# An attention and feed-forward kernel on one core: doubled temporaries and split down products in the last quarter, the weight flag made earlier, reciprocals moved to cycle heads

## The chip, the core and the metric

The kernel runs on one NeuronCore of one Trainium2 chip. A core has five engines with instruction queues of their own, worked off in order: TensorE (PE in the profile; its weight loads are listed apart as PEld), VectorE (DVE), ScalarE (ACT), GpSimd (POOL) and SyncE (SP), which here does nothing but start DMA transfers. Operands lie in SBUF, 128 partitions wide; TensorE writes its sums into eight PSUM banks of 128 x 512 fp32 each. The metric is device time in microseconds (us), the median of several runs.

## The reference

Two sequences of 1024 rows by 512 go through one layer with normalisation after each half. Cut to what matters:

```python
Q = (x @ Wq.T + bq)   # 32 heads of 16
K = (x @ Wk.T + bk)   # 8 heads of 16, each for 4 heads of Q
V = (x @ Wv.T + bv)
Q, K = _rope(Q, K)
scores = einsum('bhqd,bhkd->bhqk', Q, K) / sqrt(16)
attn = einsum('bhqk,bhkd->bhqd', softmax(scores), V)
x = _layernorm(x + attn @ Wo.T + bo)
g = einsum('th,ih->ti', x, gate_w) * gate_s      # 512 -> 1408
u = einsum('th,ih->ti', x, up_w) * up_s
hdn = silu(g) * u
x = _layernorm(x + einsum('ti,hi->th', hdn, down_w) * down_s)
```

The three feed-forward matrices hold -1, 0 and 1; the kernel checks at run time that its weights lose nothing in the matmul format, and has a general feed-forward for others.

## The kernel before, in words

**Units, steps, cycles.** The attention is cut into 32 units: sequence, half of the query rows, and group of four heads (`g`, 0 to 7). A unit has 8 steps. The main loop takes two steps at a time, so it makes 128 passes, called cycles here; a quarter (one sequence, one half of its rows) is 8 units, or 32 cycles. Operands of the score matmuls are split into a high and a low part in the matmul format, so each product is made of two matmuls.

**Two passes over the scores.** The maximum of each row of scores is needed before the exponentials. `max_pass` (L333) makes the scores once for the maximum, which VectorE takes out of a `pa` bank (L341), 12 steps ahead. `max_rows` combines these for a unit (L347 to L353: four small VectorE operations) and sends them through DRAM (L356, L359) into `mt`. `exp_pass` (L370) makes the scores again, transposed, with a third matmul that subtracts the maximum, and ScalarE takes the exponential (L378). `av` (L389) multiplies by the values, with a column of ones beside each, so that it yields numerators and denominators. After a unit's last step `unit_out` (from L399) copies the sum out, and two DMAs (L412, L413) put it into `num` and `den`. After every second unit (odd `g`) the reciprocals of `den` are taken in four pieces of 128 columns (L417), and `num` is multiplied by them (L418).

**The order.** The engines' order is written out by hand. Lists of letters (L649 to L656) say for one cycle where TensorE makes a piece of a max pass (A), of an exp pass (B), a step's value product (V, twice), and a filling block (F, at the head of a cycle): a projection with rope, or a piece of an earlier quarter's output projection or feed-forward. Cycles without a filling block use another list, and the last ones have no max pass. The four `pa` banks serve the max pass and the filling blocks by turns. `after(n, f)` puts `f` aside until n steps later; it is then issued at a V, ahead of that step's value product, in the midst of the cycle's maxima. Weight pieces are rounded and checked in the first cycles (`piece_round`, L167), at the head of a cycle.

**The weight flag.** `piece_round` gathers the low bits of all weights into `low` (the last in cycle 18). `low_flag` (L179) reduces them, sends the 128 results of 4 bytes to DRAM (`fl`, L184), back as one row (`flr`, L185), and four steps later reduces that to `flag` (L186), which is read when all else is done. `low_flag` is called at the end of cycle 26, after the load of the down weights `wd_sb` (L712, 2.8 MB) and of five weight tiles `wt` (L440) have been put on SP's queue, and before the loads `xq` of the residual rows (L429). The operand loads of a unit (`prep`, L310: KS, QH, QL) follow on the same queue at the end of every fourth cycle, three units ahead.

**A quarter's feed-forward.** Its blocks are two of `project` (two row tiles each, L463), two of `x1_turn`, then for each of 11 chunks of 128 hidden columns a gate and an up product (`hidden`, L504), then `down` for each of four row tiles (L546: 22 matmuls over the 11 chunks). A chunk's elementwise chain is: ScalarE `th` = tanh (L519) and `z` (L520); VectorE `z` = (th + 1) z (L523); ScalarE `pus` (L529), which takes the buffer of `th`; GpSimd `z` = pus z (L532); then the split into `hh` and `hl`. All of `th`, `z` and `pus` have a single buffer. Three quarters' feed-forwards fill the cycles of later attention; the last stands alone behind the loop, with eight PSUM banks, and there the split is made by ScalarE (L534) and VectorE (L535). Its `down` is followed by L555, L556, the sums (L448, L449), two small GpSimd operations (L451, L452), the norm (L458) and the store (L567).

Of the kernel before, what the change touches and what calls it, by code (L numbers as in the profile page):

```python
# [7 lines left out]
F32 = mybir.dt.float32  # L8
# [8 lines left out]
P = 128  # L17
# [29 lines left out]
def attn_ffn_kernel(tc, x, wqkv, bqkv, wo, bo, rope, wg, wu, wd, gs, us, ds, out):  # L47
    nc = tc.nc

    def pool(name, bufs=1, **kw):  # L50
        return tc.alloc_tile_pool(name=name, bufs=bufs, **kw)
# [3 lines left out]
    dram2 = pool("dram2", 2, space=DRAM)  # L55
    ap1 = pool("ap1")
    ap2 = pool("ap2", 2)
    ap3 = pool("ap3", 3)
    ap4 = pool("ap4", 4)
    wp = pool("wp", RING, side="right")  # L60
    qp1 = pool("qp1", side="right")
    qp2 = pool("qp2", 2, side="right")
# [123 lines left out]
        after(4, lambda: nc.vector.tensor_reduce(flag, flr, AX.X, ALU.max))  # L186

    later = {}
    now = [0]

    def after(n, f):
# [207 lines left out]
    def unit_out(u):  # L399


        b, qh, g = UNITS[u]
        q = u // HKV
        o = ap1.tile([P, HALF], F32, tag="o", name="o")
        nc.scalar.copy(o, PV.pop(u))
        if g % 2 == 0:
            NUM[q, g // 2] = ap4.tile([P, HALF], F32, tag="num", name="num")
            NUM["den"] = ap1.tile([P, HALF], F32, tag="den", name="den")
        num, den = NUM[q, g // 2], NUM["den"]
        r0 = (g % 2) * G * HD  # L410
        rows = slice(r0, r0 + G * HD)
        nc.sync.dma_start(out=num[rows, :], in_=o[0:P:2, :])  # L412
        nc.sync.dma_start(out=den[rows, :], in_=o[1:P:2, :])  # L413
        if g % 2:
            for k in range(TH):
                ns = slice(k * P, (k + 1) * P)
                after(min(k + 1, TH - 1), lambda ns=ns: nc.vector.reciprocal(den[:, ns], den[:, ns]))  # L417
            after(TH, lambda: nc.vector.tensor_tensor(num, num, den, ALU.mult))  # L418


    XQ, FP = {}, {}
# [76 lines left out]
    def hidden(q, f, up):  # L498
        i = (q * NF + f) * 2 + up
        w = WT.pop(i)  # L500
        p = bank("pg")
        for c in range(NC):
            for k, x1 in enumerate(FP["x1"]):
                nc.tensor.matmul(  # L504
                    p,
                    w[:, c, :],
                    x1[:, c, :],
                    start=c == 0 and k == 0,
                    stop=c == NC - 1 and k == 1,
                )  # L510
        ask_weights(i + RING - 1)
        if not up:
            if f == 0:
                FP["h"] = [
                    fp1.tile([P, NF, HALF], F32R, tag=f"h{i}", name=f"h{i}") for i in "hl"
                ]
            th = fp1.tile([P, HALF], F32, tag="th", name="th")
            z = FP["z"] = fp1.tile([P, HALF], F32, tag="z", name="z")
            nc.scalar.activation(th, p, AF.Tanh, scale=gs2[:, f : f + 1])  # L519
            nc.scalar.mul(z, p, gs2[:, f : f + 1])  # L520

            after(
                1, lambda: nc.vector.scalar_tensor_tensor(z, th, 1.0, z, ALU.add, ALU.mult)  # L523
            )
            return
        hi, lo = (h[:, f, :] for h in FP["h"])
        z = FP["z"]
        pus = fp1.tile([P, HALF], F32, tag="th", name="pus")
        nc.scalar.mul(pus, p, ust[:, f : f + 1])  # L529

        def rest():
            nc.gpsimd.tensor_tensor(z, pus, z, ALU.mult)  # L532
            if q == LASTQ:
                nc.scalar.copy(hi, z)  # L534
                nc.vector.tensor_tensor(lo, z, hi.bitcast(F32), ALU.subtract)  # L535
            else:
                nc.gpsimd.tensor_copy(hi, z)
                nc.gpsimd.tensor_tensor(lo, z, hi.bitcast(F32), ALU.subtract)

        after(1, rest)  # L540

    def down(q, t):
        pd = bank("pd")
        for f in range(NF):
            for k, h in enumerate(FP["h"]):
                nc.tensor.matmul(  # L546
                    pd,
# [2 lines left out]
                    start=f == 0 and k == 0,  # L550
                    stop=f == NF - 1 and k == 1,
                )
        ys = fp1.tile([P, D], F32, tag="ys", name="ys")
        if q == LASTQ:
            nc.vector.tensor_tensor(ys, pd, dsb, ALU.mult)  # L555
# [37 lines left out]
    def quarter(q):  # L593
# [3 lines left out]
        for f in range(NF):  # L597
            for up in (0, 1):
                fs.append(lambda a=(q, f, up): hidden(*a))
        for t in range(TH):  # L600
            fs.append(lambda t=t: down(q, t))
        return [(first, f) for f in fs]

    PHASES = 4 + 2 * NF + TH
# [59 lines left out]
    for c in range(STEPS // 2):  # L664
# [4 lines left out]
            piece_round(i)  # L669
        if pieces:  # L670
            after(1, lambda ps=pieces: [(piece_store(i), piece_load(i + 4)) for i in ps])
        alone = 2 * c + LEAD >= STEPS
        has_fill = bool(fill) and fill[0][0] <= c
        if c >= (STEPS - QS) // 2:
# [25 lines left out]
            prep(u + 3)  # L700
        if (2 * c + 1 + LEAD) % US == US - 1 and not alone:
            max_rows((2 * c + 1 + LEAD) // US)
        if c == QS // 2 - 6:
            sp4.release()
            qp4.release()
# [6 lines left out]
            nc.sync.dma_start(  # L712
                out=wd_sb.bitcast(F32), in_=wsd[2 * NF : PIECES].rearrange("f p n -> p f n")
            )
            ask_weights(RING - 1)
            low_flag()
            for t in range(TH):
                load_residual(0, t)
            for q in range(B * NH - 1):
# [1 line left out]
    for n, prob in sorted(before.items()):  # L721
        v_hook(n + 2)
        av(n, prob)
    for p in (ps_v, ps_b, ps_a[0]):
        p.release()
    ps_x = pool("ps_x", 8, space=PSUM)
    psf[0] = (ps_x, "px")

# [17 lines left out]
    fill += last[4:]  # L746
    drain()
    order.__exit__(None, None, None)
    for p in (ps_x, fp5, fp2, fp1, wp, ap4, ap3, ap2, ap1):
        p.release()  # L750
    general = nc.values_load(flag[0:1, 0:1])
    with tc.If(general != 0):
# [120 lines left out]
```

## Time and profile before

| what | us |
|---|---|
| median of 3 runs (lowest, highest) | 1245.93 (1244.38, 1246.58) |
| the profiled execution, its own time | 1244.49 |
| its span, first to last instruction | 1242.4 |
| TensorE busy | 1170.1 |
| VectorE busy | 872.4 |
| ScalarE busy | 704.7 |
| GpSimd busy | 354.1 |
| mean granted TensorE clock | 0.969 of full |

The profile is of one execution; its times are counted from the start of its span. An engine's idle time counts only where another that sets the end waits for it. The views used are the page (engine shares), the list of waits (who waited for whom), the timeline (instructions in order of time, with the idle time before each and what released it) and the view by stretches (busy time of each engine between two times, with the clock granted to TensorE). L with a number is a line of the kernel before.

### The profile page before, as it was taken

What the parts mean: (1) busy time and instruction counts of PE and PEld (TensorE: products, weight loads), DVE (VectorE), ACT (ScalarE), POOL (GpSimd) and SP (SyncE); (2) the same over time, 40 slices, a digit from 0 to 9 for tenths busy, and PEclk for the clock granted to TensorE, in tenths of its full rate; (3) what the DMA queues carried; (4) which work ended last, traced back from release to release, by engine and by line L of the source; (5) the groups of instructions that cost most, each with busy time, mean ns of one, the idle gap of its engine ahead of it and who ended that gap; (6) DMA issues with size and microseconds to landing.
All of it is one profiled execution on the core that took longest, in us unless ns stands there. A gap on an engine that the chain in (4) does not pass through costs nothing.

```text
span 1242.4 us, 22712 instructions
## 1 busy us (share of the span) xinstructions
PE 1170.1 (94%) x8784; PEld 606.5 (49%) x8784; DVE 872.4 (70%) x1492; ACT 704.7 (57%) x1300; POOL 354.1 (29%) x340
## 2 busy tenths in 40 slices
PE   7799999999799999999999999999999999999876
PEld 5344435454344454545444454546444454455664
DVE  4578898878677878785568878784867878703324
ACT  2026757566555766765446676763547776762350
POOL 3126351530103222224421222225331222245321
PEclk9679999999899999999999999999999999999897
DMA  5457776433411222221312222221212222111420
GB/s 159 130 190 252 249 233 237 155 132 122 135 44 61 79 79 81 93 78 52 99 48 67 82 92 84 84 78 44 79 60 87 78 78 79 45 61 43 136 60 36
DMA packets 82291, 126.80 MB, mean 102 GB/s; under 512 B 15873, under 2 KB 29442, under 8 KB 82050
## 3 DMA queue, kind: packets, MB, share of 16 engines
q1 hardware_dynamic: 82178, 125.30, 31.6%
q8 instruction: 71, 1.16, 0.4%
q14 instruction: 42, 0.34, 0.1%
HBM read 80.43 MB, written 36.44 MB: 94 GB/s over the span
## 4 chain that ended last, share of the span: by engine, by line
PE 62%; DVE 21%; POOL 5%; DMA 4%; issue 3%; ACT 3%; SPq 1%; POOLq 0%; DVEq 0%; ACTq 0%
PE pb L370 14%; PE pv L389 13%; DVE mx L341 12%; PE pa L333 11%; PE pg L504 10%; PE pq L241 5%; PE pd L546 5%; PE py L463 3%; DVE den L417 3%; POOL z L532 1%; DVE st L448 1%; DMA fl<-red 1%; POOL xq L561 1%; POOL ys L560 1%; DVE z L523 1%
## 5 line engine op out<-in xcount | busy, mean ns | idle before, releaser
L341 DVE TENSOR_REDUCE mx<-pa 128x1 f32<-128x512 f32 x1024 | 643.2, 681 | 187.8 <-PE pa L333 185.6
L378 ACT ACTIVATE prob<-pb 128x512 f32<-128x512 f32 x1024 | 544.5, 599 | 274.1 <-PE pb L370 263.0
L333 PE MATMUL pa<-KS,QH 32*128 32x512 f32 x1024 | 365.8, 470 | 41.7 <-DVE mx L341 23.8
L333 PE MATMUL pa<-KS,QL 32*128 32x512 f32 x1024 | 349.1, 432 | 0.0
L370 PE MATMUL pb<-QH,KS 32*128 32x512 f32 x1024 | 321.7, 477 | 1.0 <-ACT prob L378 1.0
L389 PE MATMUL pv<-prob,va 128*32 128x512 f32 x2048 | 275.5, 610 | 0.0
L370 PE MATMUL pb<-QL,KS 32*128 32x512 f32 x1024 | 270.6, 423 | 0.0
L370 PE MATMUL pb<-mt,ones 32*128 32x512 f32 x1024 | 254.5, 395 | 0.0
L333 PEld LDWEIGHTS pa<-KS,QH 32*128 32x128 f32 x1024 | 154.0, 186 | 168.7 <-DVE mx L341 144.2
L532 POOL TENSOR_TENSOR z<-pus,z 128x512 f32<-128x512 f32 x44 | 56.2, 1277 | 462.7 <-ACT pus L529 462.7
L370 PEld LDWEIGHTS pb<-QH,KS 32*128 32x128 f32 x1024 | 134.9, 182 | 82.5 <-issue 48.9
L370 PEld LDWEIGHTS pb<-QL,KS 32*128 32x128 f32 x1024 | 125.6, 184 | 85.6 <-issue 85.5
L333 PEld LDWEIGHTS pa<-KS,QL 32*128 32x128 f32 x1024 | 163.3, 188 | 5.4 <-DMA QL<-qT 0.5
L370 PEld LDWEIGHTS pb<-mt,ones 32*128 32x128 f32 x1024 | 140.6, 184 | 23.7 <-issue 15.9
L504 PE MATMUL pg<-x1h,wt 128*128 128x512 f32 x352 | 146.5, 416 | 0.7 <-ACT x1h L493 0.7
L504 PE MATMUL pg<-x1l,wt 128*128 128x512 f32 x352 | 139.5, 396 | 0.3 <-DVE x1l L494 0.3
L389 PEld LDWEIGHTS pv<-prob,va 128*32 128x32 f32 x2048 | 40.8, 108 | 93.9 <-issue 82.7
L504 PEld LDWEIGHTS pg<-x1h,wt 128*128 128x128 f32 x352 | 67.1, 191 | 38.0 <-issue 12.8
L546 PE MATMUL pd<-wd_sb,hh 128*128 128x512 f32 x176 | 71.8, 408 | 10.8 <-ACT hh L534 10.2
L241 PE MATMUL pq<-xT,wqkv_sb 128*128 128x512 f32 x160 | 76.7, 626 | 0.0
L504 PEld LDWEIGHTS pg<-x1l,wt 128*128 128x128 f32 x352 | 67.2, 191 | 13.1 <-DVE x1l L494 0.8
L546 PE MATMUL pd<-wd_sb,hl 128*128 128x512 f32 x176 | 70.5, 401 | 0.2 <-DVE hl L535 0.2
(80 smaller groups left out, 976.5 us busy)
## 6 DMA issues: line engine op xcount, KB each, us to landing
wt<-wsd SPq DMA_DIRECT2D x88, 256.0 KB
KS<-kT SPq DMA_DIRECT2D x128, 128.0 KB
wsd<-sr SPq DMA_DIRECT2D x33, 256.0 KB
qT<-hi SPq DMA_DIRECT2D x16, 512.0 KB
qT<-lo SPq DMA_DIRECT2D x16, 512.0 KB
QH<-qT SPq DMA_DIRECT2D x32, 256.0 KB
QL<-qT SPq DMA_DIRECT2D x32, 256.0 KB
xs<-in_x_dram SPq DMA_DIRECT2D x16, 256.0 KB
```

The source lines that it names most:

```text
L241: nc.tensor.matmul(pq, wqkv_sb[:, c, m * P : (m + 1) * P], XT[b, half][:, c, :], start=c == 0, stop=c == NC - 1,)
L333: nc.tensor.matmul(PA[n, j], (QH, QL)[i][u][r, t * P : (t + 1) * P], KS[u][r, half * HALF : (half + 1) * HALF], start=i == 0, stop=i == 1,)
L341: nc.vector.tensor_reduce(MX[u][:, t, j, half : half + 1], PA.pop((n, j)), AX.X, ALU.max)
L370: nc.tensor.matmul(PB[n, j], ones[r, :] if i == 2 else KS[u][r, kc * P : (kc + 1) * P], (QH[u], QL[u], mts[u % 2])[i][r, :], start=i == 0, ...
L378: nc.scalar.activation(prob[:, j, :], PB.pop((n, j)), AF.Exp, scale=SCALE)
L389: nc.tensor.matmul(PV[u][j * E : (j + 1) * E, :], vas[b][:, kc, g, :, :].rearrange("p d o -> p (d o)"), prob[:, j, :], start=done == 0, st ...
L417: after(min(k + 1, TH - 1), lambda ns=ns: nc.vector.reciprocal(den[:, ns], den[:, ns]))
L448: nc.vector.bn_stats(st, row)
L463: nc.tensor.matmul(py, NUM[q, c][:, t * P : (t + 1) * P], wo_sb[:, c, :], start=c == 0, stop=c == NC - 1,)
L504: nc.tensor.matmul(p, w[:, c, :], x1[:, c, :], start=c == 0 and k == 0, stop=c == NC - 1 and k == 1,)
L532: nc.gpsimd.tensor_tensor(z, pus, z, ALU.mult)
L546: nc.tensor.matmul(pd, h[:, f, t * P : (t + 1) * P], wd_sb[:, f, :], start=f == 0 and k == 0, stop=f == NF - 1 and k == 1,)
```

## The change

Three parts.

1. In the last quarter `th`, `z` and `pus` come from a new pool `tp2` with two buffers of each, and `pus` no longer takes the buffer of `th`. The pool lies where `ap3` (attention operands) lay, which is given back behind the main loop; for that `ap3` is made after `ap4`. The last `down` calls are cut: row tiles 0 and 1 first over chunks 0 to 9, then chunk 10 of each, then tiles 2 and 3 whole.
2. `low_flag` is called at the end of cycle 22 instead of cycle 26.
3. The reciprocals after an odd unit are issued at the heads of cycles, two at the second cycle after the unit's last value product, two at the third, and the product with `num` at the fourth. For the last unit of a quarter they stay at the steps: two at the first V after, two at the second, the product at the third (before: one, one, two, then the product at the fourth).

```diff
+    ap4 = pool("ap4", 4)
     ap3 = pool("ap3", 3)
-    ap4 = pool("ap4", 4)
...
         if g % 2:
+            c = now[0] // 2
             for k in range(TH):
                 ns = slice(k * P, (k + 1) * P)
-                after(min(k + 1, TH - 1), lambda ns=ns: nc.vector.reciprocal(den[:, ns], den[:, ns]))
-            after(TH, lambda: nc.vector.tensor_tensor(num, num, den, ALU.mult))
+                f = lambda ns=ns: nc.vector.reciprocal(den[:, ns], den[:, ns])
+                if g == HKV - 1:
+                    after(k // 2 + 1, f)
+                else:
+                    early.setdefault(c + 2 + k // 2, []).append(f)
+            f = lambda: nc.vector.tensor_tensor(num, num, den, ALU.mult)
+            if g == HKV - 1:
+                after(3, f)
+            else:
+                early.setdefault(c + 4, []).append(f)
...
-            th = fp1.tile([P, HALF], F32, tag="th", name="th")
-            z = FP["z"] = fp1.tile([P, HALF], F32, tag="z", name="z")
+            th = FP["tmp"].tile([P, HALF], F32, tag="th", name="th")
+            z = FP["z"] = FP["tmp"].tile([P, HALF], F32, tag="z", name="z")
...
-        pus = fp1.tile([P, HALF], F32, tag="th", name="pus")
+        pus = FP["tmp"].tile(
+            [P, HALF], F32, tag="pus" if q == LASTQ else "th", name="pus"
+        )
...
-    def down(q, t):
-        pd = bank("pd")
-        for f in range(NF):
+    def down(q, t, f0=0, f1=NF):
+        if f0 == 0:
+            FP["d", t] = bank("pd")
+        pd = FP["d", t]
+        for f in range(f0, f1):
...
+        if f1 < NF:
+            return
...
-        for t in range(TH):
-            fs.append(lambda t=t: down(q, t))
+        downs = [(t, 0, NF) for t in range(TH)]
+        if q == LASTQ:
+
+            downs[:2] = [(0, 0, NF - 1), (1, 0, NF - 1), (0, NF - 1, NF), (1, NF - 1, NF)]
+        for a in downs:
+            fs.append(lambda a=a: down(q, *a))
...
+        for f in early.pop(c, ()):
+            f()
         alone = 2 * c + LEAD >= STEPS
...
+        if c == QS // 2 - 10:
+            low_flag()
         if c == QS // 2 - 6:
...
+            FP["tmp"] = fp1
             ask_weights(RING - 1)
-            low_flag()
...
-    for p in (ps_v, ps_b, ps_a[0]):
+    for p in (ps_v, ps_b, ps_a[0], ap3):
         p.release()
+    FP["tmp"] = tp2 = pool("tp2", 2)
```

## The prediction

> **What bounds the kernel now.** I read the shares by engine first, then the list of waits, then the timeline at the places the change touches. TensorE is busy 94% of the span, so most of the time is matmul work that the change leaves alone; only what makes TensorE wait, or run at half clock, can be won.
>
> ```profile
> PE 1170.1 (94%) x8784; PEld 606.5 (49%) x8784; DVE 872.4 (70%) x1492; ACT 704.7 (57%) x1300; POOL 354.1 (29%) x340
> ```
>
> The list of waits (times in us: sum, count, longest):
>
> ```profile
> PE pa L333 <- DVE mx L341: 23.8, 33, 6.9
> PE pd L546 <- ACT hh L534: 10.2, 3, 3.5
> DVE flag L186 <- DMA flr<-fl: 8.3, 1, 8.3
> ```
>
> The reader is to see two waits of TensorE and one wait of VectorE that feeds the first: of its 23.8 us, 6.9 are one wait. I call one pass of the main loop a cycle (128 of them). A cycle ends with every eighth `mt,ones` matmul in TensorE's timeline, so the timeline gives each cycle's length.
>
> *The tail.* One chunk of the last feed-forward in the timeline (start, duration, engine, line; in brackets the idle time before it and its releaser):
>
> ```profile
> 1170.73 0.68 ACT L519 ACTIVATE th<-pg,gs 128x512 f32<-128x512 f32 x1
> 1171.58 0.69 ACT L520 ACTIVATE z<-pg,gs 128x512 f32<-128x512 f32 x1 [0.17 <-DVE hl L535]
> 1172.30 0.69 DVE L523 SCALAR_TENSOR_TENSOR z<-th,z 128x512 f32<-128x512 f32 x1 [0.76 <-ACT z L520]
> 1173.09 0.69 ACT L529 ACTIVATE pus<-pg,ust 128x512 f32<-128x512 f32 x1 [0.82 <-DVE z L523]
> 1173.92 1.29 POOL L532 TENSOR_TENSOR z<-pus,z 128x512 f32<-128x512 f32 x1 [3.75 <-ACT pus L529]
> 1175.24 0.62 ACT L534 CAST hh<-z 128x512 fp32r<-128x512 f32 x1 [1.46 <-POOL z L532]
> 1175.77 0.68 ACT L519 ACTIVATE th<-pg,gs 128x512 f32<-128x512 f32 x1
> ...
> 1206.12 0.49 PE L546 MATMUL pd<-wd_sb,hh 128*128 128x512 f32 x1 [3.19 <-ACT hh L534]
> ```
>
> A chunk takes 5.04 us here (1170.73 to 1175.77), while its 16 matmuls start 0.227 us apart and need 3.63. TensorE ends the hidden layer at 1199.15, then finds chunks 8 to 10 missing, waits, and falls to half clock.
>
> *The flag, and the middle.* First the timeline, then the view by stretches, cut at cycle ends (from:to, length, busy time of each engine, granted clock, DMA share, GB/s):
>
> ```profile
> 324.21 0.27 DVE L186 TENSOR_REDUCE flag<-flr 1x1 int32<-1x128 int32 x1 [8.27 <-DMA flr<-fl]
> ```
>
> ```profile
> 303.10:312.20 9.10, 8.30 (x61) 3.79 (x62) 7.27 (x13) 4.36 (x8) 0.00 (x0) 0.81 0.95 335
> 318.20:333.60 15.40, 8.49 (x61) 4.02 (x62) 6.77 (x12) 4.34 (x8) 4.97 (x4) 0.67 0.56 154
> ...
> 428.10:436.20 8.10, 7.55 (x67) 3.66 (x65) 7.96 (x16) 4.92 (x10) 3.16 (x3) 1.00 0.02 4
> 443.70:451.00 7.30, 7.30 (x67) 3.79 (x65) 5.18 (x10) 5.48 (x11) 3.17 (x3) 1.00 0.61 182
> 1199.00:1219.00 20.00, 9.61 (x28) 6.02 (x27) 6.11 (x9) 8.37 (x13) 5.08 (x4) 0.69 0.00 0
> ```
>
> Cycles 27 and 29 take 9.1 and 15.4 us at a reduced clock where their neighbours take 5.95. Cycle 42, with two reciprocals and the product, takes 8.10 where a plain one takes 7.29.
>
> **Part 1, the tail.** The single `th` buffer, shared with `pus`, makes L529 wait for L523, and the single `z` makes L520 wait for L535. With two buffers each and `pus` apart, both waits go. The in-order ScalarE loop stays: from T, the start of `th`: `z` at T+0.58 (1160.10 to 1160.68, the one place without the wait), L523 at T+1.30 (0.72 after `z`, as above), its end T+1.99, L532 0.14 later (the gap from L529's end to L532), `hh` 1.32 after that at T+3.45, next `th` 0.53 later: 3.98 us a chunk instead of 5.04. `th` of chunk 1 starts at 1165.68 in both, so chunk 9 starts at 1165.68 + 8 x 3.98 = 1197.5 and chunk 10 at 1201.5; `hl` ends 4.8 us after `th`, at 1202.3 and 1206.3.
>
> TensorE's hidden matmuls do not wait now, so the downs begin at 1199.15 as before. In the new order, tile 0 over chunks 0 to 9, tile 1 likewise, then chunk 10 of each: chunk 9 is wanted at 1199.15 + 18 x 0.227 = 1203.2 (there at 1202.3), chunk 10 at 1199.15 + 40 x 0.227 = 1208.2 (there at 1206.3). No wait, hence no half clock: 88 matmuls end their starts at 1218.9 instead of 1233.6, 14.7 us earlier. The order costs something behind it: tiles 0 and 1 now finish together, at 1208.9, and each takes VectorE 3.95 us of L555, L556, sums and norm; tile 2 starts at 1216.8, tile 3 at 1220.7 instead of the 1219.3 when its matmuls are done. From L555 of tile 3 to the end is 8.4 us now (1234.03 to 1242.4), so the end is 1229.1: **13.3 us won**. If the loop stayed near 4.3 us, TensorE would wait about 2: 11; 14.7 is the other end. That the tile pool lies on freed attention buffers costs nothing: their readers ended at 1125.
>
> **Part 2, the flag.** Before, `fl` is issued at 306.9 behind 4.1 MB of `wd_sb` and `wt`, SP waits 13.8 us for it, and `flr` wakes VectorE at 324.2; behind L186 stand the maxima, behind them TensorE. In the new program `red` stands at the end of cycle 22, `fl` and `flr` go out near 279.5 with an idle queue, and L186 comes 13 maxima after `red`, 9.7 us later (1.6 cycles of 5.95), near 288.7. Only the loads of KS, QH and QL for unit 8 stand behind on SP, wanted at 296. Ready when? `flr` took 2.9 us from issue to L186. For `fl` the trace shows 14.4 us behind the queue, and its last packets some 5 us before SP goes on. The row gives about 5.6 + 2.9, ready at 288.3, just in time. The Trainium skill (DMA: Bandwidth & Descriptors, "Latency and other measured facts", with "Specifications" on read-modify-write below 512 B) puts most of some 2 us a transfer in the receipt of the write: ready at 284, no wait. I take the row, and 0.3 us for `red` and a short wait.
>
> What is late next: without SP's 13.8 us wait, the `xq` loads follow `wt` at 307, and then KS, QH and QL of unit 9, for which cycle 30 waits. Their data follow 4.1 MB that end at 315.2; `xq` and these 2.1 MB and a 0.26 MB `o` took 9.0 us from the first packet at 322.5 to 331.5, some 7.5 of it in a full queue: there at about 323. Cycle 30 would start on its own at 322 to 324 (from 296.4: cycle 26 at 7.2, since row maxima and two reciprocals, 2.48, meet a slack of some 1.2; the next three at 6.5, 6.05, 5.95; 2.2 more if the clock drops in 27 as now). So it starts near 323.8 instead of 333.6: 9.8 less the 0.3, **9.5 us won** (6 if the loads come late and stall the clock again, 11.5 if neither happens). This contains the reciprocals of cycles 26 to 28.
>
> **Part 3, the reciprocals.** 64 of 0.93 us, as many as before: only place counts. Now they stand among the maxima at each V; afterwards, with c the cycle of the unit's last value product, two at the head of cycle c+2, two of c+3, the product at c+4. At a head VectorE is idle while TensorE does the filling block: 1.61 us with a hidden block (L341 idle at 423.23), 3.1 with a projection. Two reciprocals take 1.67 (432.31 to 433.98).
> - Eight odd units beside hidden blocks (cycles 42, 50, ...): now 0.16 + 0.81 over plain cycles of 7.48 and 7.29. The first head also holds the row maxima (0.81, 430.34 to 431.15), put there at the end of the cycle before: 2.48 into 1.61, 0.87 late, of which about 0.25 is slack. So 0.6 stays and 0.36 is won: **3.0 us** with the ninth, whose second cycle has no maxima (0.16). Ends: nothing, or all 7.9.
> - Units 1 and 3, beside projections: now cycles 9 and 10 take 10.19 and 10.17, 17 and 18 take 9.34 and 10.16, against 8.87: 4.4 over. New heads: 0.81 + 1.38 (two `low`) + 1.67 = 3.86 into 3.1 once, the others fit. **3.5 us won** (2 to 4.4).
> - Each quarter's last unit (cycles 33, 65, 97) has no filling block; its reciprocals move half a cycle earlier, two at each V. Now these two cycles take 0.7 over; two bunched pairs should cost 0.3 more each: **0.9 lost** (none to 3).
>
> Here a rule speaks about the price of such stalls. The clock record drops to half at 305.63 for 3.4 us, in cycle 27, although TensorE's longest wait around it is 0.70. By the Trainium skill (TensorE: Matmul & The Clock Gate, "HAM oscillation") only idle gaps over some 3.4 us drop it. By the rule the stalls of part 3 cost only themselves; by this row each can cost about 2.4 more. But 14 units with stalls of 0.2 to 0.9 elsewhere kept clock 1.00, so I add nothing beyond cycle 27.
>
> **Sum.** 13.3 + 9.5 + 3.0 + 3.5 - 0.9 = 28.4. The profiled execution took 1244.49 (span 1242.4 and 2.1 around it), 1.44 below the median of the runs: 1216.1 for such an execution, **1217.5** for a median.
>
> **Rivals.**
> - *The loads take the flag's gain* (0.12): cycle 30 waits for KS and QH and the clock halves. For it: 4 MB lie ahead in the queue. Against: my count leaves them 1 us. Part 2 is worth 4: 1223.
> - *The heads help nothing* (0.10): row maxima and reciprocals together stall TensorE as much as now, and the last units lose 3: part 3 is worth -3: 1226.
> - *The heads hide everything* (0.06): 7.9 + 4.4 and no loss: 1211.
> - *Slower* (0.02): every head with row maxima and reciprocals halves the clock for one window, as in cycle 27. 14 places at 2.4 us are 34, against 28 won: 1251. It decides from the twelfth place on; the record shows none at such a stall but one.
>
> **Chances.** The forecast as worked out has 0.70, with 1213 to 1222 as its own range from the ends of its terms. To leave out no more than 2 in 10 the range goes to both neighbours: 1210 to 1226. About 0.2%, 2.5 us, is what a measurement of this kernel can tell from no change. Every case but the last is faster by more: 0.97; 0.01 for within, a mix of losses; 0.02 slower.
>
> **What would show it.** Right: `th` to `th` near 3.98 us in the last feed-forward, no TensorE wait for `hh`, full clock from 1150 to the end of the downs; L186 without idle time, cycle 29 near 6; heads with two reciprocals ahead of the first maximum and cycle 42 at 7.8 to 7.9. Wrong: TensorE waiting for QH or KS near cycle 30; half-clock windows at cycles 10, 26, 33, 42; tile 3's L555 well behind its last matmul by more than 1.5.

## The result, and the profile after

| | median (lowest to highest), us | runs |
|---|---|---|
| before | 1245.21 (1244.38 to 1246.58) | 4 |
| changed | 1232.06 (1230.99 to 1235.38) | 4 |

The ratio is 0.990, with a 95% interval of 0.9875 to 0.9921. The changed kernel is 13.1 us faster by the medians, 12.7 by the ratio. The forecast was 28.4 us, and the time lies outside the range of 1210 to 1226: the direction was right, and a good half of the gain did not come. (Profiled execution of after: 1231.15, span 1229.3, mean clock 0.973.) In the profiles of after, line numbers are those of the changed file: L334 for the max pass, L342 for its maximum, L419 for the reciprocals, L424 for the product with `num`, L529 to L560 for the feed-forward.

The shares by engine of after:

```profile
PE 1174.0 (96%) x8784; PEld 611.6 (50%) x8784; DVE 875.3 (71%) x1492; ACT 704.4 (57%) x1300; POOL 353.2 (29%) x340
```

TensorE's busy time went up by 3.9 us with the same 8784 matmuls: some of them now run at half clock that did not before. The list of waits of after:

```profile
PE pa L334 <- DVE mx L342: 15.0, 23, 1.7
DVE flag L186 <- DMA flr<-fl: 1.9, 1, 1.9
```

The wait for `hh` in the tail is gone from this list, the wait for the maxima fell from 23.8 to 15.0, and the flag's from 8.3 to 1.9. So the waits that the change aimed at are gone or shorter; most of the loss is elsewhere. First the tail, one chunk and the first two row tiles of the last feed-forward in the timeline of after:

```profile
1170.24 0.68 ACT L529 ACTIVATE th<-pg,gs 128x512 f32<-128x512 f32 x1
1170.82 0.68 ACT L530 ACTIVATE z<-pg,gs 128x512 f32<-128x512 f32 x1
1171.39 0.69 ACT L541 ACTIVATE pus<-pg,ust 128x512 f32<-128x512 f32 x1
1171.53 0.69 DVE L533 SCALAR_TENSOR_TENSOR z<-th,z 128x512 f32<-128x512 f32 x1 [0.47 <-ACT z L530]
1172.39 1.28 POOL L544 TENSOR_TENSOR z<-pus,z 128x512 f32<-128x512 f32 x1 [2.72 <-DVE z L533]
1173.71 0.62 ACT L546 CAST hh<-z 128x512 fp32r<-128x512 f32 x1 [1.63 <-POOL z L544]
1174.23 0.69 ACT L529 ACTIVATE th<-pg,gs 128x512 f32<-128x512 f32 x1
...
1209.43 0.69 DVE L571 TENSOR_TENSOR ys<-pd,dsb 128x512 f32<-128x512 f32 x1 [2.35 <-PE pd L560]
1213.25 0.68 DVE L571 TENSOR_TENSOR ys<-pd,dsb 128x512 f32<-128x512 f32 x1
```

A chunk takes 3.99 us (1170.24 to 1174.23); 3.98 was worked out. Row tile 0 starts its closing work at 1209.43 (1208.9 forecast), row tile 3 at 1220.88 (1220.7 forecast). The stretches of after, in the columns of those before, show where the gain went:

```profile
290.50:299.32 8.82, 8.21 (x60) 3.81 (x62) 6.40 (x11) 4.37 (x8) 0.00 (x0) 0.81 0.38 113
307.19:314.18 6.99, 6.72 (x59) 3.13 (x58) 6.50 (x11) 4.36 (x8) 0.00 (x0) 1.00 1.03 383
351.50:362.54 11.04, 9.71 (x57) 3.92 (x56) 8.43 (x17) 4.36 (x8) 0.00 (x0) 0.69 0.03 4
425.70:433.50 7.80, 7.71 (x65) 3.79 (x65) 7.30 (x16) 5.00 (x10) 3.16 (x3) 1.00 0.08 17
620.90:631.00 10.10, 8.29 (x58) 3.70 (x56) 8.90 (x18) 4.38 (x9) 0.00 (x0) 0.83 0.03 5
889.50:899.00 9.50, 8.21 (x56) 3.53 (x56) 8.26 (x17) 4.34 (x8) 0.00 (x0) 0.82 0.02 4
1199.00:1219.00 20.00, 20.00 (x90) 16.54 (x89) 10.15 (x18) 4.09 (x7) 4.15 (x6) 1.00 0.07 27
```

The last row is the tail: TensorE busy throughout, at full clock, where before it was busy 9.61 of 20 us at 0.69. The second is cycle 27, now 6.99; the fourth is cycle 42, 7.8 where it was 8.1, as forecast. But four cycles have a granted clock of 0.69 to 0.83 that had 1.00 before: cycle 25 (the first row) and cycles 34, 66 and 98, the second after each quarter's last unit. In the clock record of after, the half-clock windows are at 292.30, 353.74, 623.40 and 893.05, one in each of these cycles, and one at 1155.88 that before has as well. For comparison, the stretch of before that holds cycle 34:

```profile
357.90:364.60 6.70, 6.45 (x56) 2.75 (x56) 6.56 (x14) 4.35 (x9) 0.00 (x0) 1.00 0.04 7
```

Summed over cycles, the two profiled executions compare like this (minus is won):

| where | forecast | measured |
|---|---|---|
| tail, from the end of cycle 127 | -13.3 | -13.1 |
| flag, cycles 25 to 30 | -9.5 | -6.5 |
| units beside hidden blocks | -3.0 | -2.8 |
| units 1 and 3 | -3.5 | -3.0 |
| last units of quarters, cycles 34, 66, 98 | +0.9 | +10.6 (4.4, 3.4, 2.8) |
| cycle 64, half clock in the execution before alone | none | -1.5 |
| start-up, to the end of cycle 0 | none | +3.4 |
| rest | none | -0.2 |
| sum | -28.4 | -13.1 |

The start-up has the same instructions in both. TensorE reached full clock at 8.67 us before and at 15.8 after. I set this down as a difference between two executions, not as part of the change: in the fourteen profiles of this document cycle 0 ends between 83 and 88 us, in no order that fits the edits. Cycle 64 is of the same kind. It or cycle 96 holds a half-clock window in seven of the fourteen profiles, of the kernel before and of variants alike, at 1.5 to 2.9 us each. Where cycle 64 keeps full clock, cycle 66 takes 7.4 us and not 6.7 even without any change to the last units; so some 0.7 of its 3.4 belongs to cycle 64.

### The profile page after: what moved, and what is told of

Read it like the earlier page. It is cut to its first block, busy times and chain, and to the rows that moved or that the text cites. A ratio compares the mean times of both kernels' runs of the same rounds, so it can differ in the third digit from the quotient of the medians.

```text
span 1229.3 us, 22709 instructions
## 1 busy us (share of the span) xinstructions
PE 1174.0 (96%) x8784; PEld 611.6 (50%) x8784; DVE 875.3 (71%) x1492; ACT 704.4 (57%) x1300; POOL 353.2 (29%) x340
## 3 DMA queue, kind: packets, MB, share of 16 engines
q8 instruction: 71, 1.16, 0.4%
## 4 chain that ended last, share of the span: by engine, by line
PE 73%; DVE 17%; DMA 3%; POOL 3%; issue 2%; ACT 1%; SPq 0%; POOLq 0%; DVEq 0%; ACTq 0%
PE pb L371 16%; PE pv L390 16%; PE pg L514 13%; PE pa L334 12%; DVE mx L342 9%; PE pq L242 5%; PE pd L560 5%; PE py L473 4%; DVE den L419 3%; DVE st L458 1%; POOL xq L577 1%; POOL ys L576 1%; ACT prob L379 1%; DMA fl<-red 1%; PE pv L293 1%
## 5 line engine op out<-in xcount | busy, mean ns | idle before, releaser
L342 DVE TENSOR_REDUCE mx<-pa 128x1 f32<-128x512 f32 x1024 | 644.5, 682 | 183.7 <-PE pa L334 179.6
L334 PE MATMUL pa<-KS,QH 32*128 32x512 f32 x1024 | 364.9, 469 | 33.6 <-DVE mx L342 15.0
L334 PE MATMUL pa<-KS,QL 32*128 32x512 f32 x1024 | 350.5, 433 | 0.1
L371 PE MATMUL pb<-QH,KS 32*128 32x512 f32 x1024 | 318.1, 475 | 1.0 <-ACT prob L379 1.0
L371 PE MATMUL pb<-QL,KS 32*128 32x512 f32 x1024 | 273.5, 421 | 0.0
L334 PEld LDWEIGHTS pa<-KS,QH 32*128 32x128 f32 x1024 | 152.8, 187 | 157.9 <-DVE mx L342 131.9
L334 PEld LDWEIGHTS pa<-KS,QL 32*128 32x128 f32 x1024 | 162.9, 189 | 5.7 <-DMA QL<-qT 0.9
L514 PEld LDWEIGHTS pg<-x1l,wt 128*128 128x128 f32 x352 | 67.1, 191 | 13.1 <-DVE x1l L504 0.8
L560 PE MATMUL pd<-wd_sb,hh 128*128 128x512 f32 x176 | 69.9, 397 | 0.7 <-ACT o L406 0.7
L560 PE MATMUL pd<-wd_sb,hl 128*128 128x512 f32 x176 | 68.6, 390 | 0.0
```

What stands on the lines that cost most here:

```text
L334: nc.tensor.matmul(PA[n, j], (QH, QL)[i][u][r, t * P : (t + 1) * P], KS[u][r, half * HALF : (half + 1) * HALF], start=i == 0, stop=i == 1,)
L342: nc.vector.tensor_reduce(MX[u][:, t, j, half : half + 1], PA.pop((n, j)), AX.X, ALU.max)
L371: nc.tensor.matmul(PB[n, j], ones[r, :] if i == 2 else KS[u][r, kc * P : (kc + 1) * P], (QH[u], QL[u], mts[u % 2])[i][r, :], start=i == 0, ...
L514: nc.tensor.matmul(p, w[:, c, :], x1[:, c, :], start=c == 0 and k == 0, stop=c == NC - 1 and k == 1,)
L560: nc.tensor.matmul(pd, h[:, f, t * P : (t + 1) * P], wd_sb[:, f, :], start=f == 0 and k == 0, stop=f == NF - 1 and k == 1,)
```

## The experiments

In the expectations, theory A says that the two pairs of reciprocals in a quarter's last cycles hold up TensorE by about a microsecond, that this halves its clock, and that this is where most of the missing gain went. B is its rival: half-clock windows fall by chance, where the window of the clock happens to begin, so that the pairs cost only their own stall. Each group of runs has its own runs of the kernel before on the same chip (medians 1247.2, 1245.1 and 1244.6). Gains below are (1 - ratio) x 1245 us, with the interval worked out likewise.

### One part alone, or one piece undone

**The last units' reciprocals put back**, everything else as changed:

```diff
-                    after(k // 2 + 1, f)
+                    after(min(k + 1, TH - 1), f)
...
-                after(3, f)
+                after(TH, f)
```

> The changed kernel with one thing undone: after the last unit of each quarter the reciprocals go out one, one, two at the next three Vs and the product at the fourth, as before. Theory A: two reciprocals at each V overrun the four banks, TensorE waits over 1 us within one clock window and the clock halves; the three cycles 34, 66 and 98, now 11.0, 10.1 and 9.5 us, go back to about 6.7, so the kernel is 10.6 us under the changed one, some 24 under before (about 1221), with no half-clock window at these places. Theory B: the half-clock windows fall where the free-running window happens to begin, wherever VectorE works; then some of these drops stay or move, and the gain is the stall alone, 1 us a place: about 1229.

Measured: 1220.37 (1218.69 to 1224.36), ratio 0.9790 (0.9770 to 0.9809): 26.1 us under before, with an interval that doesn't touch the changed kernel's. The stretches of this kernel at the first two of the three places:

```profile
347.50:354.30 6.80, 6.70 (x60) 3.33 (x60) 6.66 (x14) 4.38 (x9) 0.00 (x0) 1.00 0.03 5
614.70:622.10 7.40, 6.87 (x56) 2.93 (x57) 7.26 (x15) 4.37 (x9) 0.00 (x0) 1.00 0.03 7
```

Full clock, and 6.8 and 7.4 us instead of 11.0 and 10.1. By the medians this piece cost the change some 13 us. Not all of that is its own: the two profiles are 12.5 us apart, of which 9.9 stand in the three cycles and 1.6 in cycle 25, where the flag's wait, 1.84 us here, cost no clock this time (7.23 us instead of 8.82).

**The flag read two steps later**, everything else as changed:

```diff
-        after(4, lambda: nc.vector.tensor_reduce(flag, flr, AX.X, ALU.max))
+        after(6, lambda: nc.vector.tensor_reduce(flag, flr, AX.X, ALU.max))
```

> The changed kernel with one thing changed: the flag is read six steps after it is asked for, not four. In the changed kernel VectorE waits 1.9 us for the row in cycle 24, and a half-clock window follows. If that wait is the cause, cycle 25 goes from 8.8 back to 5.95 us, and the kernel is about 2.9 under the changed one (1229). If the window is chance, the wait goes but a window stays near there: 1.0 to 1.9 gained or nothing.

Measured: 1232.10 (1227.02 to 1235.72), ratio 0.9883 (0.9862 to 0.9903), 14.6 us under before. The medians don't tell it from the changed kernel (12.7), so its worth stays uncertain. Its profile does show the wait gone. From the timeline and, below, a stretch over cycle 25 and the head of cycle 26 of this kernel:

```profile
293.28 0.26 DVE L186 TENSOR_REDUCE flag<-flr 1x1 int32<-1x128 int32 x1
```

```profile
290.00:296.40 6.40, 6.40 (x64) 3.22 (x58) 5.49 (x12) 4.63 (x9) 0.00 (x0) 1.00 0.52 145
```

L186 has no idle time before it, cycle 25 is back at 5.95 us and the clock is 1.00. Cycles 34 and 98 keep their losses (11.09 and 9.50 us); cycle 66 takes 8.30 us, at full clock, which is taken up below.

**Part 1 alone.** Edit: parts 2 and 3 of the diff left out.

```diff
-                if g == HKV - 1:
-                    after(k // 2 + 1, f)
-                else:
-                    early.setdefault(c + 2 + k // 2, []).append(f)
...
+                after(min(k + 1, TH - 1), lambda ns=ns: nc.vector.reciprocal(den[:, ns], den[:, ns]))
+            after(TH, lambda: nc.vector.tensor_tensor(num, num, den, ALU.mult))
...
-        if c == QS // 2 - 10:
-            low_flag()
...
+            low_flag()
```

> Part 1 alone; flag and reciprocals as before. By the step of the prediction, 13.3 under before (about 1232); the profile of the changed kernel says 12.8 between the end of cycle 127 and the end. If the rest of the change mattered for the tail, it would be less.

Measured: 1233.48 (1230.97 to 1235.44), ratio 0.9882 (0.9863 to 0.9901): 14.7 us, 12.3 to 17.1. The forecast of 13.3 holds. The tail alone is worth as much as the whole change.

**Part 3 alone.** Edit: the kernel before, with these lines of the diff and the loop over `early` at the head of a cycle.

```diff
-                after(min(k + 1, TH - 1), lambda ns=ns: nc.vector.reciprocal(den[:, ns], den[:, ns]))
-            after(TH, lambda: nc.vector.tensor_tensor(num, num, den, ALU.mult))
+                if g == HKV - 1:
+                    after(k // 2 + 1, f)
+                else:
+                    early.setdefault(c + 2 + k // 2, []).append(f)
+            f = lambda: nc.vector.tensor_tensor(num, num, den, ALU.mult)
+            if g == HKV - 1:
+                after(3, f)
+            else:
+                early.setdefault(c + 4, []).append(f)
```

> Part 3 alone; tail and flag as before. From the cycles of the changed kernel: units 1 and 3 give 3.1, the nine beside hidden blocks 3.2, the three last units cost 10.6 under theory A, cycles 25 to 27 about even: 4 us slower than before (1249). Theory B, drops by chance: 3 to 5 us faster (1241).

Measured: 1251.97 (1246.61 to 1259.62), ratio 1.0043 (1.0023 to 1.0063): 5 us slower than before, as theory A has it. Cycles 34, 66 and 98 take 9.54, 10.15 and 10.95 us in its profile. This profile also has half clock in cycle 96, for 2.9 us, one of the chance windows named above. So the pairs cost more than the cycle heads win, with neither of the other parts in the kernel.

**Part 2 alone.**

```diff
+        if c == QS // 2 - 10:
+            low_flag()
         if c == QS // 2 - 6:
...
-            low_flag()
```

> Part 2 alone; tail and reciprocals as before. Cycle 29 loses 9.4 us, cycle 27 most of its 3.2 (the clock drop there came with the reduction of the flag), cycle 25 gains up to 2.9 for the late row, cycle 30 gains 1 for the loads of unit 9: 7 to 10 under before. If the loads took the whole gain, 4.

Measured: 1242.41 (1237.32 to 1244.99), ratio 0.9973 (0.9961 to 0.9985): 3.4 us, not 9.5, and near the 4 of the rival in which the loads take the gain. Cycle 29 fell from 15.40 to 5.95 us, and cycle 30 rose from 6.27 to 11.10. The half clock that stood in cycle 27 came in cycle 26 here (the two take 6.70 and 9.11 us before, 9.30 and 6.34 now), which won nothing. The stretches, cycles 29 and 30:

```profile
321.80:327.70 5.90, 5.90 (x54) 2.78 (x49) 4.91 (x9) 4.34 (x8) 5.00 (x4) 1.00 1.03 272
327.70:338.80 11.10, 9.84 (x62) 4.18 (x63) 5.91 (x13) 4.35 (x8) 0.00 (x0) 0.69 0.06 14
```

And the timeline at the head of cycle 30 of this kernel:

```profile
328.71 0.21 DVE L353 STREAM_TRANSPOSE mr<-mm 128x32 f32<-128x32 f32 x1
328.96 0.70 PE L333 MATMUL pa<-KS,QH 32*128 32x512 f32 x3 [1.26 <-DVE mr L353]
329.58 0.18 PEld L333 LDWEIGHTS pa<-KS,QL 32*128 32x128 f32 x1 [0.31 <-DMA QL<-qT]
```

The DMA engines are full through cycle 29 (share 1.03) and idle in cycle 30 (0.06): the loads end at the boundary. TensorE's first matmul of the new unit, which reads KS and QH, waits 1.26 us, then the next weight load waits for QL. The profile puts the first wait down to `mr` (L353), but a score matmul doesn't read `mr`; a later experiment (below) settles that it is the loads. The clock halves from 330.1 for two windows.

The parts' medians add up: 14.7 + 3.4 - 5.3 = 12.8, against 12.7 for the change, with intervals of 1.5 to 2.9 us either way. It does not follow that the parts leave each other alone: in the profiles cycles 25 to 30 win 3.8 us with the flag alone, 0.2 with the reciprocals alone and 6.5 with both. That the sum comes out so well is partly luck.

### Is it the pairs, and the clock?

The timeline of the changed kernel around the first of the three places, VectorE's work and TensorE's wait:

```profile
347.57 1.75 DVE L419 RECIPROCAL den<-den 128x128 f32<-128x128 f32 x2
349.24 1.22 DVE L342 TENSOR_REDUCE mx<-pa 128x1 f32<-128x512 f32 x2
350.38 1.76 DVE L419 RECIPROCAL den<-den 128x128 f32<-128x128 f32 x2
352.05 1.82 DVE L342 TENSOR_REDUCE mx<-pa 128x1 f32<-128x512 f32 x3
...
352.73 1.08 PE L334 MATMUL pa<-KS,QH 32*128 32x512 f32 x2 [1.23 <-DVE mx L342]
```

Between 347.57 and 352.05 VectorE takes only two maxima (1.22 us); the four reciprocals take 3.5 us of it, the time of five more. The `pa` banks come free late, TensorE waits 1.23 us, and at 353.74 its clock halves for 6.8 us. All of the record's changes begin and end on a grid of 3.41 us; in the grid window before this one TensorE was idle 1.33 us in sum.

**The pairs kept, only the product put back** to the fourth V:

```diff
-                after(3, f)
+                after(TH, f)
```

> The changed kernel with only the product of the last units put back to the fourth V; their reciprocals stay two at each V. Theory A (the pairs overrun the banks): TensorE still waits over 1 us in cycles 33, 65 and 97, cycles 34, 66 and 98 stay at 9.5 to 11, and the kernel is within 2 us of the changed one (13 to 15 under before). Rival: the product, moved half a cycle ahead onto the row maxima, is what tips it; then those cycles go back to 6.7 and it is about 24 under before.

Measured: 1229.67 (1223.11 to 1234.92), ratio 0.9864 (0.9827 to 0.9901). Cycles 34, 66 and 98 still take 9.53, 10.95 and 9.53 us, with half-clock windows at 354.6, 624.2 and 897.3. The product isn't the cause; the pairs are.

**Counting the places.** The pairs stand at three places in each of four profiles: the changed kernel, the one with the flag read later, part 3 alone, and this one. At all twelve TensorE waits 1.2 to 1.7 us in one piece, and at eleven the clock halves at the first line of the grid after the wait. The twelfth is cycle 66 with the flag read later. Its timeline, then its stretch:

```profile
619.98 1.09 PE L334 MATMUL pa<-KS,QH 32*128 32x512 f32 x2 [1.23 <-DVE mx L342]
```

```profile
618.00:626.30 8.30, 6.98 (x59) 3.13 (x57) 8.16 (x17) 4.35 (x9) 0.00 (x0) 1.00 0.03 5
```

A line of that execution's grid, at 619.10, cuts the wait into 0.34 and 0.88 us. The clock stayed full, and the cycle took 8.30 us where the kernel before has 6.67: the stall alone costs about 1.6. Three of the other eleven waits were cut too, but each left 1.0 us or more in the later window. So B is right in one thing: how the grid happens to lie can decide whether the clock's price comes on top of the stall. The ten profiles without the pairs have one half-clock window at their thirty such places (cycle 66 of the kernel with one reciprocal at each V, below).

**Pairs put where there were none.** To the kernel with both faults mended (the next group), cycle 31 gets two reciprocals of a buffer of ones at each V, and the first V of cycle 32 two products. This is useless extra work, and nothing reads its results.

```diff
...
+    def two():
+        for k in range(2):
+            nc.vector.reciprocal(dm[:, k * P : (k + 1) * P], dm[:, k * P : (k + 1) * P])
+    later.setdefault(62, []).append(two)
+    later.setdefault(63, []).append(two)
+    for _ in range(2):
+        later.setdefault(64, []).append(lambda: nc.vector.tensor_tensor(dm, dm, dm, ALU.mult))
```

> The kernel with both mended, and useless work put in: two reciprocals of a dummy tile at each V of cycle 31, two products of it at the first V of cycle 32, where both cycles took 5.95 and 6.06 us with nothing to stall them. Theory A (bunched VectorE work overruns the banks, and the wait halves the clock): half-clock windows begin in cycle 31 or 32, and the two cycles take 3 to 5 us more. Theory B (half-clock windows fall by chance): the cycles take about 1 us more, with no half-clock window begun there.

Measured: 1221.78 (1220.58 to 1228.42), ratio 0.9832 (0.9800 to 0.9864). Its profile has the same picture at the new place. The timeline, then the stretches of cycles 31 and 32:

```profile
335.14 1.75 DVE L688 RECIPROCAL dm<-dm 128x128 f32<-128x128 f32 x2
337.49 1.08 PE L334 MATMUL pa<-KS,QH 32*128 32x512 f32 x2 [1.32 <-DVE mx L342]
```

```profile
330.20:336.20 6.00, 5.97 (x56) 2.79 (x52) 6.00 (x10) 4.36 (x8) 0.00 (x0) 1.00 0.01 3
336.20:345.90 9.70, 8.32 (x62) 3.69 (x62) 8.52 (x14) 4.83 (x9) 0.00 (x0) 0.82 0.40 120
```

A wait of 1.32 us, the clock halved from 339.69 for one window, and 9.72 us for cycle 32, which takes 6.06 without the dummy work. Of these 3.7 us the wait itself is about a third; most of the rest goes with the clock. The kernel's median does not show the cost: it is 20.9 us under before, with an interval that overlaps that of the same kernel without the dummy work (25.0), and the two profiles are equally long, since cycles 30 and 64 happened to lose less in this one. What shows it is the place: the wait and the half clock came where the work was put. Together with the twelve places above, this shows that the bunched work causes the wait and that the clock follows it as a rule.

### What is left of the missing gain

**Both faults mended**: the two diffs at the start of these experiments together.

> The changed kernel with both: the last units' reciprocals as before, and the flag read six steps after it is asked for. With the first alone the kernel was 26 us under before, and its profile still had 1.3 us over in cycle 25. Expected 27.5 to 29 under before, near the 28.4 that the prediction summed up.

Measured: 1219.77 (1217.73 to 1221.49), ratio 0.9799 (0.9773 to 0.9825), 25.0 us under before, 2 to 4 less than expected, and no better than the last units' piece alone (26.1; the intervals overlap). Cycles 25, 34, 66 and 98 are whole again, but cycle 64 has a chance drop (9.98 us, 7.1 without one), and cycle 30 takes 10.43. Its head in the timeline of this kernel:

```profile
321.89 0.95 PE L334 MATMUL pa<-KS,QH 32*128 32x512 f32 x3 [0.73 <-DVE neg L348]
322.50 0.28 PEld L334 LDWEIGHTS pa<-KS,QL 32*128 32x128 f32 x1 [0.30 <-DMA QL<-qT]
```

The same kind of wait as with the flag alone, and the clock halves from 322.17 for two windows.

**The down weights loaded later**: both faults mended, and the 2.8 MB of `wd_sb` issued at the end of cycle 28 instead of 26, behind the operands of unit 9.

```diff
+        if c == QS // 2 - 4:
+            nc.sync.dma_start(
+                out=wd_sb.bitcast(F32), in_=wsd[2 * NF : PIECES].rearrange("f p n -> p f n")
+            )
...
-            nc.sync.dma_start(
-                out=wd_sb.bitcast(F32), in_=wsd[2 * NF : PIECES].rearrange("f p n -> p f n")
-            )
```

> The kernel with both mended, and the 2.8 MB load of the down weights put off by two cycles, from the end of cycle 26 to the end of cycle 28, behind the operand loads of unit 9. If TensorE waits for QH and QL at the head of cycle 30, and the clock halves by that wait, cycle 30 goes from 10.4 (both mended) or 7.3 (changed kernel) to 6.3, and the kernel is 1 to 4 us under the one with both mended. If the wait in cycle 30 is the row maxima (the releaser that the profile names), cycle 30 stays above 7.

Measured: 1215.49 (1214.99 to 1217.32), ratio 0.9766 (0.9749 to 0.9783): 29.1 us under before (27.0 to 31.2). The stretches of cycles 29 and 30:

```profile
316.30:322.20 5.90, 5.90 (x59) 3.04 (x56) 4.92 (x9) 4.35 (x8) 0.00 (x0) 1.00 0.86 289
322.20:328.50 6.30, 6.30 (x60) 3.11 (x58) 5.66 (x13) 4.37 (x9) 0.00 (x0) 1.00 0.59 216
```

TensorE is busy without a gap through both, and between the start-up and 1141 us the clock record has no half-clock window at all. Only the order of loads was changed, and the wait at the head of cycle 30 went: it was the loads, not `mr`. Cycle 30 takes 6.26 us instead of 10.43. The medians are 4 us apart, but their intervals overlap, and cycle 64 alone differs by 2.9 us, through its chance drop; so the gain of this edit rests on cycle 30. The version is 16 us under the changed one. That it reaches the forecast's 28.4 says nothing for the forecast: it is another kernel.

**One reciprocal at each V** for the last units and unit 5, on both faults mended; the product at the head of the next cycle.

```diff
-                if g == HKV - 1:
-                    after(min(k + 1, TH - 1), f)
+                if g == HKV - 1 or u == 5:
+                    after(k + 1, f)
...
+            elif g == HKV - 1 or u == 5:
+                early.setdefault(c + 3, []).append(f)
```

> Both mended, and in cycles without a filling block the reciprocals one at each V (last units, and unit 5 in cycles 25 and 26), with the product at the head of the next cycle. If single reciprocals are free there, as cycles 25 and 33 of the kernel before say (5.94 and 5.97 against 5.95), cycles 34, 66 and 98 go from 6.7 to about 6.1 and cycles 26 and 27 from 7.9 and 7.0 to about 6.2 each: 4 us under the kernel with both mended, 32 under before. If the banks are overrun by the sum of the work and not by its bunching, no gain.

Measured: 1222.63 (1218.89 to 1226.72), ratio 0.9828 (0.9793 to 0.9864). The expected gain didn't come. For the last units spreading changed nothing: cycles 34 and 98 take 6.69 and 6.68 us, as with both faults mended (6.67 and 6.69), and cycle 66 has a half-clock window (8.48). For unit 5 a new wait took its place, seen in this kernel's timeline:

```profile
294.64 0.95 DVE L419 RECIPROCAL den<-den 128x128 f32<-128x128 f32 x1 [2.57 <-DMA den<-o]
296.20 0.50 PE L334 MATMUL pa<-KS,QH 32*128 32x512 f32 x1 [1.23 <-DVE mx L342]
```

For unit 5 the first reciprocal now comes before `den` has landed. SP waited 7.1 us for `fl`; behind that stood the operand loads of the next unit, and behind them the load of `den`. VectorE, which works in order, held its maxima for 2.57 us; TensorE waited 1.23 and the clock halved from 296.6.

### The two halves of part 1

**Doubled temporaries without the split downs**, parts 2 and 3 left out:

```diff
-        if q == LASTQ:
-
-            downs[:2] = [(0, 0, NF - 1), (1, 0, NF - 1), (0, NF - 1, NF), (1, NF - 1, NF)]
```

> Of part 1 the doubled temporaries alone; the last down products in their old order. Chunk 10 is there at 1206.3 on the clock of the prediction and wanted at 1199.15 + 20 x 0.227 = 1203.7: TensorE waits 2.6 us in tile 0, then runs on, and the tiles end one after another, so that VectorE has no queue: tile 3 is done 2.6 us later than in the changed kernel and starts on VectorE 1.2 us later: 12 under before, if the clock stays full; 10 if it halves for a window.

Measured: 1235.56 (1233.71 to 1237.85), ratio 0.9920 (0.9903 to 0.9937): 10.0 us. The timeline:

```profile
1209.77 0.50 PE L551 MATMUL pd<-wd_sb,hh 128*128 128x512 f32 x1 [1.98 <-ACT hh L537]
```

TensorE finds chunk 10 missing for 1.98 us, and the clock halves at 1210.5 for one window.

**Split downs with single temporaries**, parts 2 and 3 left out:

```diff
-            [P, HALF], F32, tag="pus" if q == LASTQ else "th", name="pus"
+            [P, HALF], F32, tag="th", name="pus"
...
-    FP["tmp"] = tp2 = pool("tp2", 2)
+    FP["tmp"] = fp1
```

> Of part 1 the split of the down products alone; temporaries single as before. The chain still takes 5.04 us a chunk and ends at 1216.8; by then tiles 0 and 1 are done but for chunk 10, and 48 matmuls are left where before 70 were: 22 x 0.227 = 5 us gained, a little more or less by the clock: 4 to 6 under before.

Measured: 1241.12 (1240.02 to 1244.86), ratio 0.9976 (0.9966 to 0.9986): 3.0 us, a little under what was expected. One stretch of the tail:

```profile
1202.00:1222.50 20.50, 13.62 (x44) 9.80 (x43) 4.84 (x7) 8.54 (x14) 5.09 (x4) 0.75 0.00 1
```

The chain still gives a chunk each 5.04 us, so TensorE starves whatever the order. Alone they are worth 10.0 and 3.0; together 14.7 (12.3 to 17.1). Nothing shows that together they are worth more than the sum: in the profiles the tail is 10.4 and 2.8 us shorter with one of them, and 13.1 to 14.3 in the nine kernels with both. Behind the doubled temporaries the split removes the wait for chunk 10 and, with it, the clock window.

## Why the prediction was right in part and wrong in its sum

- **The tail** was right: 13.3 forecast, 13.1 in the profile, 14.7 (12.3 to 17.1) alone on the chip. The chunk time and the starts of the closing work by row tile came out as worked out from the chain's gaps. One sign was set wrong: "full clock from 1150" holds in neither kernel, since both have two half-clock windows from about 1156 on; after them, from 1162.7, the clock of the changed kernel was full to the end of the downs.
- **The odd units** were right: beside hidden blocks seven of the eight take 0.13 us less in the first cycle and 0.25 less in the second, the 0.36 of the working; the eighth won nothing (cycle 114 takes 8.18, not 7.83). That makes 2.8 against 3.0, and 3.0 against 3.5 for units 1 and 3.
- **"0.9 lost" for each quarter's last unit** is the step that failed: measured were 10.6 in the table, and 9.9 against the profile with these reciprocals put back. The mechanism was in the working, that two bunched pairs hold up the maxima, but both terms of its price were wrong. The stall was put at 0.3 a place; where the clock stayed full it cost 1.6. The clock was put at nothing ("so I add nothing beyond cycle 27"); it halved at all three places and took the rest, by estimate 5 us (9.9 less three times 1.6).

  On the clock the text had weighed the rule of the Trainium skill (TensorE: Matmul & The Clock Gate, "HAM oscillation"), idle gaps over some 3.4 us, against the row of cycle 27, a drop with no wait over 0.70, at about 2.4 us each. That only such gaps lower the clock does not hold here: waits of 1.2 to 1.7 us did. By the row, three places at 0.3 + 2.4 come to 8.1. The row was right that the clock has a price; that its sum comes near the measured one is partly luck, since its stall was too small and its 2.4 more than the 1.7 a place of the estimate.

  I argued the row away with 14 units whose stalls of 0.2 to 0.9 cost no clock. Most of those have a filling block in the cycle, and the last units among them left TensorE idle for only 0.25 us of cycle 34 (the stretch of before above). Now it waits 1.23 us in one piece there, in a cycle without a filling block. Whether the block is what saves the others no run settles.
- **"9.8 less the 0.3" for the flag** failed at two terms. The first is `fl`: 5.6 us was taken out of a trace in which it stood behind a full queue. (The sum 279.5 + 5.6 + 2.9 is 288.0, where the text has 288.3; nothing hangs on it.) The timeline of after, with the queue idle:

```profile
279.43 0.34 SPq L184 DMA_DIRECT2D fl<-red  x1
287.32 0.23 SPq L185 DMA_DIRECT2D flr<-fl  x1
290.08 0.27 DVE L186 TENSOR_REDUCE flag<-flr 1x1 int32<-1x128 int32 x1 [1.89 <-DMA flr<-fl]
```

  It takes 7.9 us from one issue to the next, and 2.8 for `flr`. L186 so waits 1.89 us, and instead of 0.3 this costs 2.9 in cycle 25, since the clock halves there as well; with nearly the same wait and full clock it cost 1.3 (the last units' reciprocals put back). The estimate of 284 by the Trainium skill (DMA: Bandwidth & Descriptors, "Latency and other measured facts") would have been further off still: the row landed at 290.1. The second is "what is late next". The loads of unit 9 were named, with a slack of 1 us at the head of cycle 30, and the forecast took them as just hidden. They were not: with the flag alone the wait of 1.26 us and two half-clock windows took 4.8 back in cycle 30. That is the rival given 0.12, and it priced part 2 at 4 against 3.4 measured. In the changed kernel itself cycle 27 is 0.6 us longer, the wait is 0.56 and the clock stayed full; only 1.1 was taken back.
- **The slower rival**, every head with row maxima and reciprocals halving the clock, was wrong about its place: no such head did so. A like price, at three other places, is what took the gain.

What stays open: why the clock halves at one wait and not at another. How the grid cuts the wait is one part, as cycle 66 showed. It is not all: in the changed kernel the clock fell after grid windows with 0.62, 1.33, 1.81 and 1.16 us of idle TensorE, and stayed full after others with up to 1.02; in other profiles it fell after a window with 0.1 (cycle 25 with the product put back) and stayed full after one with 1.32 (cycle 9, with a filling block, of the doubled temporaries alone). The chance windows of cycles 64 and 96 come under the same heading.

## What to carry to other kernels

Before work is bunched on the engine that frees TensorE's buffers, count how long it keeps that engine from freeing them, and price the stall by what the trace shows a clock drop to cost, not by its own length alone: here waits of 1.2 to 1.7 us stood in cycles that became 2.8 to 4.4 us longer, and 1.6 where the clock stayed full. A clock drop in the trace of before that no rule explains is a price to use, not an exception to argue away. When a wait on a queue is taken out, everything behind it moves up and competes: what then decides is the order of the loads on the queue, worth 4.2 us in cycle 30 here for one moved DMA. And one profile's total holds chance clock windows of 1.5 to 2.9 us, so a piece is better read cycle by cycle.

## What the runs showed of the hardware that was not expected

- In all fourteen profiles TensorE's clock changes only on a grid of 3.41 us, which lies differently in each execution; the free-running window of that length is in the Trainium skill (TensorE: Matmul & The Clock Gate, "Part 1"), and the record's changes agree with it. What the runs add is how little idle time in such a window can be enough. In the cycles of 32-row tiles into which work was bunched, the clock halved after each of the twelve windows with 1.1 to 1.8 us of idle TensorE, the one made on purpose among them, and stayed full after the one with 0.98. This is no threshold for other cycles, as the windows with 0.1 and 1.32 us show.
- Sending 128 results of 4 bytes each to DRAM took 7.1 to 7.9 us on an idle queue before the DMA that reads them was issued (nine profiles); reading them back as one row took 2.8 to 3.2 (the four in which VectorE waited for it).
